# Four edits to a four-layer graph network on one core: fixed PSUM banks in attention, blocks prepared later, last rows tile by tile, source scores on the sync queue

## The chip, the cores and the metric

The kernel runs on one core of a Trainium2 chip. The metric is the device time of one execution in microseconds (us). The engines are named as in the profile: PE (matmuls; PEld is its loading of weights), DVE (vector), ACT (scalar), POOL (GpSimd) and SP (sync). SP, ACT and Pool issue DMAs; an engine issues in program order, so an instruction that waits on an engine's sequencer holds all that are behind it there.

## What is computed

`x` is 4096 x 256 and `adj` 4096 x 4096, all f32. Four layers follow each other, each with a residual and a layernorm:

```python
x = layernorm(x + attention(x, adj))   # 4 heads of 64: softmax(q k^T * 64**-0.5 + gb * adj, masked where adj == 0) v, then Wout, bout
x = layernorm(x + gat(x, adj))         # Wh = x W; e = leaky(es[i] + ed[j], 0.2), masked where adj <= 0; softmax(e) Wh
x = layernorm(x + (d adj d x) W2^T + b2)   # d = rowsum(adj)**-0.5
x = layernorm(x + relu((d adj d x) W3))
```

In layer 1, es = Wh a[:256] is the score of the source (the row) and ed = Wh a[256:] that of the target.

## The kernel before, in words

**Order of the work.** The program fixes the order of instructions on each engine (a manual schedule): every engine works through its instructions as the Python code issues them. Waits between engines and on DMAs are put in from the tiles that are read and written.

**Layer 0** takes the span from 72 to 1290 us. It goes through 64 units: 32 blocks of 128 rows, each with two pairs of heads. A unit has eight scores and eight turns, which `section` issues by the string `ORDER = "HHTHTHTTHHTHTHTT"` (L43). H is `score` (L447): for 512 columns, one matmul for each of the two heads (PE L451, with K of 64, into two PSUM banks; the profile has an f32 matmul as two records, so four for a score), and DVE L459 evicts each bank, adding the bias (edges and mask) and taking the maximum `mx` as it goes. T is `turn` (L482): 16 transposes on PE (L489) of 1024 columns of the unit *before* into two banks, which ACT L496 evicts. After the fourth H, `sums` (L515) takes the reciprocal of the exponentials' sums (DVE L519), transposes it (L527) and sends it through DRAM by two DMAs on Pool. `maxima` ends the section. Then `columns` (L600) issues what goes by unit or block: `begin` (L390, q of the next block), `finish` (L417, the output projection of the block before), `spread`, `attend` (L501; PE L505, 32 matmuls of 128 columns for each of the two heads, into the bank `po`), the exponentials (`expo`, ACT L474) and `make_bias` of the next block (DVE). `scale` (L557), first in a section, takes the result of `attend` of the unit before the last out of `po`.

PSUM has eight banks. Seven (`NB`) go round: `next_bank` (L228) and `next_two` (L233) hand them out in a fixed rotation to scores, turns, `begin` and `finish`. The eighth is `po` (L220), for `attend` alone. The last unit is turned in `drain` (L800), outside of `section`.

**Layer 1** lies between about 1314 and 1795 us. It has 32 units of 128 rows, each in four steps: 128 steps in all. A step has 32 rows, whose 4096 columns lie as four quarters of 1024 on the 128 partitions. `gat_step(t)` (L1080) issues for step t: the score of step t (DVE: `mask_out` L174 on the mask, from unit 1 on, then L996, which adds ed and takes the maximum), the leaky function of step t-2 (ACT L1008, with `es_q` as its bias), the exponential of t-5 (ACT L1037), the turn of t-6 (DVE L1045, a 32 x 32 transpose) and the attention of t-10 (`attend`, PE L1056: eight accumulating matmuls of 257 columns, 16 records, 3.47 us on PE). Every fourth step also folds the maxima of a unit (ACT L1015, DVE L1020 to L1027, ACT L1034). In its first steps PE has project_w (L176: Wh and the scores; PE L182, ACT L190 copies the result out), which a table `filling` (L1144 to L1158) spreads over steps 1 to 8. The same table has at steps 2, 5, 7 and 10 `take_es` (L192; DVE L193 copies source scores to `esd`) and `send_es` (L1119): it stores a part of `esd` to DRAM (`e_src`, L1121) and loads it back in another layout to the four quarters of `es_q` (L1123, four DMAs, which read what the store wrote). At step 5 `load_rows` (L1128) loads x into `xc` (8 x 512 KB, SP), and from step 4 on, each unit's `load_masks` (L158; L164, 8 x 128 KB, SP) is issued as the unit begins, at t = 4u. `load_last_weights` is at step 12. SP waits only for buffers to come free and for data that it reads, so these loads run ahead of the steps as far as the buffers allow.

**Layers 2 and 3** (about 1795 to 2609 us) multiply by adj in 64 steps each (`T1` = 64; 16 for each of four column blocks). A step has seven products (`product`, PE L1255, 14 records, 6.01 us a step), of sums and differences of blocks: `sums(t+1)` makes those of adj one step ahead (DVE L1199 to L1202, 2.94 us), and `prepare(p, layer)` (L940) those of x for a pair p of row blocks: layernorm (DVE L149), scaling (ACT L947), sums (DVE L950, L953, L954). When a column block ends, `keep` evicts seven banks, `combine` (L1266) adds them up on DVE in the next two steps, and `hidden_sums` (L1294) does sums on Pool. A table `at_step` gives the steps of these. For layer 3, `prepare(p, 1)` is put at the later of two steps: r0 + 4 + s, when the rows of p are through layer 2, and `free` = 48 + p + 6, when the storage that it writes is free; so p = 10 and 11 come at steps 64 and 65 and p = 12 at step 73.

**The end** (`end`, L1355) is the last column block: after the last products, eight tiles of 128 rows (n = 0 to 7) are multiplied by W3 (`weigh`, two halves f), put through relu (ACT L1383), added to x (`onto_x`, L1385), given statistics (`stats`), rates (`rates`, L1412, four tiles together), applied (`apply`) and stored in four DMAs (`put`, L1407).

Of the kernel before, what the change touches and what calls it, by code (L numbers as in the profile page):

```python
# [17 lines left out]
P = 128  # L18
# [22 lines left out]
MASK0 = -1.0e9  # L41
NB = 7
ORDER = "HHTHTHTTHHTHTHTT"  # L43

MASK1 = -4.5e16
SLOPE = 0.2
# [3 lines left out]
def tile_gnn(  # L50
# [165 lines left out]
    with ExitStack() as l0:  # L216
        ps = ExitStack()
        ps_b = ps.enter_context(tc.tile_pool(name="l0banks", bufs=1, space=PSUM))
        banks = [ps_b.tile([P, BJ], F32, name=f"bank{b}") for b in range(NB)]
        po = ps_b.tile([P, BJ], F32, name="po")  # L220

        rp = l0.enter_context(tc.tile_pool(name="l0raw", bufs=2))
        big = l0.enter_context(tc.tile_pool(name="l0big", bufs=1))
# [90 lines left out]
        class Rows:  # L314
# [73 lines left out]
                nc.sync.dma_start(self.xr, x[i0 : i0 + P, :])  # L388

            def begin(self):  # L390
                pq = next_bank()
                self.qT = wk2.tile([P, 2, P], F32, tag="qT", name="qT")
                for pr in range(2):
                    for cc in range(2):
                        for j in range(2):
                            h = 2 * pr + j
                            nc.tensor.matmul(  # L397
                                pq[j * HD : (j + 1) * HD, pr * P : (pr + 1) * P],
                                wq_sb[:, cc, h * HD : (h + 1) * HD],
                                self.xq[:, cc, :],  # L400
                                start=(cc == 0),
                                stop=(cc == 1),
                            )
# [11 lines left out]
                nc.gpsimd.tensor_tensor(self.xr, self.xr, bout_b, ALU.add)  # L415

            def finish(self):  # L417
                pp = next_bank() if self.ib + 1 < NCH else banks[NB - 1]
                for pr in range(2):
                    for j in range(2):  # L420
                        nc.tensor.matmul(  # L421
                            pp[j * HD : (j + 1) * HD, 0:D],
                            self.oT[:, pr, j * HD : (j + 1) * HD],
                            wout_sb[:, pr, :],
                            start=(pr == 0),
                            stop=(pr == 1),
                        )
                nc.vector.tensor_reduce(
                    rowsum[:, self.ib : self.ib + 1], self.rs, AX.X, ALU.add
                )  # L430
                nc.vector.tensor_tensor(self.xr, pp[:, 0:D], self.xr, ALU.add)
                ln_stats(wk2, self.xr, self.ib)
                if self.ib + 1 < NCH:
                    nc.sync.dma_start(x0_pre[self.ib * P : (self.ib + 1) * P, :], self.xr)

        class Unit:
# [7 lines left out]
                self.nm = wk2.tile([P, 2], F32, tag="nm", name="nm")  # L444
                self.ls = wk2.tile([P, 2], F32, tag="ls", name="ls", bufs=3)

            def score(self, m):  # L447
                ps = next_two()
                m0 = m * BJ
                for j in range(2):  # L450
                    nc.tensor.matmul(  # L451
                        ps[j],
                        self.rows.qT[j * HD : (j + 1) * HD, self.pr, :],
                        kT[j * HD : (j + 1) * HD, self.pr, m0 : m0 + BJ],
                        start=True,
                        stop=True,
                    )
                for j in range(2):
                    nc.vector.tensor_tensor_reduce(  # L459
                        self.z[j][:, m0 : m0 + BJ],  # L460
                        ps[j],
                        self.rows.bias[m0 // TS][:, m0 % TS : m0 % TS + BJ],
                        1.0,
                        NEG,
                        ALU.add,
                        ALU.max,
                        self.mx[:, j, m : m + 1],
                    )
# [10 lines left out]
                    accum_out=self.ls[:, j : j + 1],  # L479
                )  # L480

            def turn(self, k, j, by_dve=False):  # L482

                pa = next_two()
                z = self.z[j][:, k * TS : (k + 1) * TS]
                for c in range(CS):
                    for r in range(2):
# [13 lines left out]
            def attend(self, c0=0, c1=NCH):  # L501
# [10 lines left out]
                if c1 == NCH:  # L512
                    self.z = None

            def sums(self):  # L515

                u = self.u
                l2 = wk2.tile([P, 2], F32, tag="l2", name="l2")
                nc.vector.reciprocal(l2, self.ls)  # L519
# [53 lines left out]
        def section(u):  # L573
# [5 lines left out]
            h = t = 0  # L579
            if u >= 2:  # L580
                units.pop(u - 2).scale()
            for op in ORDER:
                if op == "H":
                    unit.score(h)
                    if h == 3:
                        before.sums()
                    h += 1
                else:
                    before.turn(t % NS, t // NS)
                    if t == 3:  # L590
                        give_edges()
                    t += 1
# [207 lines left out]
        def drain():  # L800
# [1 line left out]
            unit = units[last]  # L802

            def turn(k, j):
                unit.turn(k, j, by_dve=(j == 0))

            units[last - 1].scale()
            turn(0, 0)
            turn(1, 0)
            turn_part(0)  # L810
            load_part(7)
            unit.sums()
            rows[-1].add_bout()
            turn(0, 1)
# [36 lines left out]
        if True:  # L851
# [24 lines left out]
            load_next(0, 0)  # L876
            units[0] = Unit(0)
            for m in range(NH):
                units[0].score(m)
                if m < NH - 2:  # L880
                    project_v(m)
                if m % 2 == 0 and m < NH - 2:
# [92 lines left out]
    with ExitStack() as l1:  # L975
# [142 lines left out]

        def send_es(b0, b1):  # L1119

            nc.gpsimd.dma_start(e_src[:, b0:b1], esd[:, b0:b1])  # L1121
            for q in range(NA):
                nc.gpsimd.dma_start(  # L1123
                    es_q[q * QB : (q + 1) * QB, :, b0:b1],
                    e_src.rearrange("(a r) b -> r a b", r=QB)[:, :, b0:b1],
                )
# [49 lines left out]
    with ExitStack() as l2:  # L1176
# [51 lines left out]
        class Block:  # L1228
# [126 lines left out]
            def end(self, t0):  # L1355
# [23 lines left out]
                def onto_x(n):  # L1379
# [1 line left out]
                    ci = h * NP + self.jb * NSJ + s  # L1381
                    r = wk.tile([P, D], F32, tag="relu", name="relu")
                    nc.scalar.activation(r, py[n][:, 0:D], AF.Relu, scale=d3[:, ci : ci + 1])  # L1383
                    eng = nc.vector if n > NSJ and n % 2 else nc.gpsimd
                    eng.tensor_tensor(xc[:, ci, :], xc[:, ci, :], r, ALU.add)  # L1385

                def stats(n):
# [56 lines left out]
                for n in range(NSJ):  # L1444
                    onto_x(n)
                    stats(n)
                for n, tag in zip(range(NSJ, 2 * NSJ), ("m6", "m1", "m5", "y")):
                    weigh(n, tag, (0,))
                rates(0)
                for n in range(NSJ, 2 * NSJ, 2):  # L1450
                    for i in range(n, n + 2):
                        weigh(i, None, (1,))
                        onto_x(i)
                    stats(n)
                    stats(n + 1)
# [29 lines left out]
        with tc.manual_schedule():  # L1485
# [5 lines left out]
            for t in range(n_all):  # L1491
# [20 lines left out]
                if c == NP - 1:  # L1512
# [72 lines left out]
```

## Time and profile before

| what | us |
|---|---|
| runs | 2630.45, 2631.6, 2631.25 (median 2631.25) |
| profiled execution | 2627.84 |
| its span | 2626.1 |
| mean granted clock of PE | 0.999 |
| layer 0's units | 72 to 1290, 19.45 each |
| layer 1's steps | 1314 to 1795 |
| layers 2 and 3 | 1795 to 2609 |

The span is the time from the first to the last instruction or transfer that the profile records; the execution's own time is 1.7 us longer. The profile is one execution, by itself 3.4 us faster than the median of the runs. How to read its views:

- Busy time: each engine's busy microseconds, their share of the span and the number of instructions.
- Chain: the work that ended last, followed back from the end, at each step to what released it; a piece is its start, its length up to the start of the next piece, and engine, tile and line.
- Waits: who waited for whom, in us in all, how often, and the longest.
- Timeline: start, length, engine, line, operation, tiles (written <- read), shape, how many; in brackets the idle time before and what ended it. SPq and ACTq are DMA issues of these engines' sequencers.
- DMA issues: who issues, how many, the size of each and the median time from issue to landing, such as these of before:

```profile
mk<-edge SPq DMA_DIRECT2D x256, 128.0 KB, 2.9
x_pre<-xr SPq DMA_DIRECT2D x31, 128.0 KB, 1.7
es_q<-e_src POOLq DMA_DIRECT2D x8, 2.0 KB, 5.1
e_src<-esd POOLq DMA_DIRECT2D x2, 2.0 KB, 5.0
```

### The profile page before, as it was taken

What the parts mean: (1) busy time and instruction counts of PE and PEld (TensorE: products, weight loads), DVE (VectorE), ACT (ScalarE), POOL (GpSimd) and SP (SyncE); (2) the same over time, 40 slices, a digit from 0 to 9 for tenths busy, and PEclk for the clock granted to TensorE, in tenths of its full rate; (3) what the DMA queues carried; (4) which work ended last, traced back from release to release, by engine and by line L of the source; (5) the groups of instructions that cost most, each with busy time, mean ns of one, the idle gap of its engine ahead of it and who ended that gap; (6) DMA issues with size and microseconds to landing.
All of it is one profiled execution on the core that took longest, in us unless ns stands there. A gap on an engine that the chain in (4) does not pass through costs nothing.

```text
span 2626.1 us, 59453 instructions
## 1 busy us (share of the span) xinstructions
PE 2612.5 (99%) x24058; PEld 1829.7 (70%) x24058; DVE 2203.3 (84%) x4709; ACT 1555.6 (59%) x2195; POOL 471.6 (18%) x743
## 2 busy tenths in 40 slices
PE   9999999999999999999999999999999999999998
PEld 5777778778787787777888888885444444444444
DVE  5999999999999999999789898886966688777676
ACT  2999999999999999999877667661100001010011
POOL 0122221221222212212720000001222021121120
PEclk9999999999999999999999999999999999999999
DMA  6444544545545445454472222213544545445543
GB/s 159 89 99 91 103 94 96 102 92 98 97 94 99 97 95 103 90 100 95 155 206 76 73 78 81 73 65 113 176 158 163 170 154 172 160 160 189 173 160 111
DMA packets 678292, 312.39 MB, mean 119 GB/s; under 512 B 552096, under 2 KB 582688, under 8 KB 678016
## 3 DMA queue, kind: packets, MB, share of 16 engines
q1 hardware_dynamic: 655968, 264.97, 40.3%
q0 software_dynamic: 20096, 42.05, 4.9%
q8 instruction: 188, 3.08, 0.5%
q10 hardware_dynamic: 1952, 1.58, 0.2%
q14 instruction: 88, 0.72, 0.1%
HBM read 262.40 MB, written 46.09 MB: 117 GB/s over the span
## 4 chain that ended last, share of the span: by engine, by line
PE 98%; DVE 1%; DMA 0%; ACT 0%; POOL 0%; issue 0%; DVEq 0%; POOLq 0%; ACTq 0%
PE m L1255 29%; PE bank L451 18%; PE po L505 17%; PE po L1056 17%; PE bank L489 10%; PE py L1305 2%; PE bank L397 1%; PE bank L421 1%; PE bank L298 1%; PE bank L277 1%; PE sc L182 0%; DMA e_src<-esd 0%; DMA es_q<-e_src 0%; PE ped L744 0%; PE po L268 0%; PE py L1286 0%
## 5 line engine op out<-in xcount | busy, mean ns | idle before, releaser
L459 DVE CUSTOM_DVE_ANT_0 z<-bank,bias 128x512 f32<-128x512 f32 x1024 | 646.4, 687 | 53.5 <-PE bank L451 49.6
L496 ACT COPY z<-bank 128x512 f32<-128x512 f32 x1016 | 535.1, 598 | 109.5 <-PE bank L489 102.3
L451 PE MATMUL bank<-store,qT 64*128 64x512 f32 x2048 | 535.4, 619 | 0.0
L474 ACT ACTIVATE z<-z,nm 128x4096 f32<-128x4096 f32 x128 | 475.7, 3738 | 1.1 <-DVE nm L471 1.1
L489 PEld LDWEIGHTS bank<-ident,z 64*128 64x128 f32 x8192 | 338.1, 139 | 178.4 <-issue 136.0
L505 PE MATMUL po<-z,xc 128*64 128x128 f32 x8192 | 458.4, 273 | 0.0
L505 PEld LDWEIGHTS po<-z,xc 128*64 128x64 f32 x8192 | 450.2, 137 | 4.8
L1056 PE MATMUL po<-store,pt 128*128 128x257 f32 x2048 | 445.3, 379 | 0.0
L1056 PEld LDWEIGHTS po<-store,pt 128*128 128x128 f32 x2048 | 387.5, 189 | 57.7
L1255 PE MATMUL m<-asum,ysum 128*128 128x512 f32 x672 | 324.8, 592 | 1.9 <-DVE asum L1199 1.9
L489 PE MATMUL bank<-ident,z 64*128 64x64 f32 x8192 | 318.8, 222 | 0.7 <-DVE xt L695 0.3
L1255 PEld LDWEIGHTS m<-asum,ysum 128*128 128x128 f32 x672 | 127.6, 190 | 162.5 <-issue 144.5
L451 PEld LDWEIGHTS bank<-store,qT 64*128 64x128 f32 x2048 | 168.0, 187 | 76.2 <-issue 54.9
L1255 PE MATMUL m<-asum,store 128*128 128x512 f32 x448 | 210.7, 592 | 0.0
L1255 PE MATMUL m<-a,ysum 128*128 128x512 f32 x448 | 210.6, 592 | 0.0
L1045 DVE STREAM_TRANSPOSE pt<-z 128x1024 f32<-128x1024 f32 x128 | 158.1, 1237 | 37.9 <-PE po L1056 32.3
L1199 DVE TENSOR_TENSOR asum<-a,a 128x512 f32<-128x512 f32 x128 | 93.4, 730 | 105.7 <-PE m L1255 105.7
L374 POOL DMA_DIRECT2D edge<-mk x128 | 74.0, 578 | 578.1 <-ACT mk L368 565.4
L354 DVE SCALAR_TENSOR_TENSOR bias<-rt,gb,u 128x1024 f32<-128x1024 f32 x128 | 164.5, 1285 | 4.5
L1318 ACT COPY e<-py 128x512 f32<-128x512 f32 x28 | 16.4, 586 | 250.1 <-PE py L1305 172.9
L339 DVE STREAM_TRANSPOSE rt<-raw 128x1024 f32<-128x1024 f32 x128 | 158.6, 1239 | 5.9 <-DMA raw<-in_adjT 5.5
L1200 DVE TENSOR_TENSOR asum<-a,a 128x1024 f32<-128x1024 f32 x128 | 162.2, 1267 | 0.0
(201 smaller groups left out, 2774.6 us busy)
## 6 DMA issues: line engine op xcount, KB each, us to landing
a<-in_adjT SPq DMA_DIRECT2D x256, 512.0 KB, 4.8
raw<-in_adjT SPq DMA_DIRECT2D x512, 128.0 KB, 3.9
edge<-mk POOLq DMA_DIRECT2D x128, 256.0 KB, 3.2
mk<-edge SPq DMA_DIRECT2D x256, 128.0 KB, 2.9
xq<-in_xT SPq DMA_DIRECT2D x32, 128.0 KB, 3.6
xr<-in_x SPq DMA_DIRECT2D x32, 128.0 KB, 3.7
x<-xs POOLq DMA_DIRECT2D x8, 512.0 KB, 6.1
xc<-x SPq DMA_DIRECT2D x8, 512.0 KB, 10.1
```

The lines of the kernel that those rows point to most:

```text
L339: nc.vector.transpose(rt.rearrange("p (b r) -> p b r", r=QB), self.raw.pop(k))
L354: nc.vector.scalar_tensor_tensor(b, self.turned[0], gb, self.u, ALU.mult, ALU.add)
L451: nc.tensor.matmul(ps[j], self.rows.qT[j * HD : (j + 1) * HD, self.pr, :], kT[j * HD : (j + 1) * HD, self.pr, m0 : m0 + BJ], start=True, s ...
L459: nc.vector.tensor_tensor_reduce(self.z[j][:, m0 : m0 + BJ], ps[j], self.rows.bias[m0 // TS][:, m0 % TS : m0 % TS + BJ], 1.0, NEG, ALU.add ...
L474: nc.scalar.activation(self.z[j], self.z[j], AF.Exp, bias=self.nm[:, j : j + 1], accum_out=self.ls[:, j : j + 1],)
L489: nc.tensor.transpose(pa[r][:, c * HD : (c + 1) * HD], z[half, c * P : (c + 1) * P], ident[half, half],)
L496: copy(z.rearrange("p (c r i) -> p r c i", r=2, i=HD)[:, r, :, :], pa[r].rearrange("p (c i) -> p c i", i=HD),)
L505: nc.tensor.matmul(po[j * HD : (j + 1) * HD, 0:P], v_sb[:, ci, h * HD : (h + 1) * HD], self.z[j][:, ci * P : (ci + 1) * P], start=(ci == 0 ...
L1045: nc.vector.transpose(self.pt[:, :, s, :], self.z[:, s, :].rearrange("p (b r) -> p b r", r=QB))
L1056: nc.tensor.matmul(self.po[:, 0 : D + 1], self.pt[:, b, :, :].rearrange("p s i -> p (s i)"), wh[:, b, :], start=(b == 0), stop=(b == NBK - 1),
L1200: nc.vector.tensor_tensor(s[:, 0:2, :], a0, a1, ALU.add)
L1255: nc.tensor.matmul(self.m[i], left, right, start=(c == 0), stop=(c == NP - 1))
```

## The change

1. Layer 0: `po` becomes the eighth of `banks`. The 16 operations of a section take their two banks from a table, `PLACES`; `begin` and `finish` take bank 6 (`SIDE`), except `begin` of the first block. The first unit and `drain` keep the rotation of seven. The reciprocal of `sums` becomes a method of its own, `reciprocals`, issued after the second H.
2. Layer 3's `prepare` that `free` would put on steps 64 to 66 comes three steps later, at 67 and 68 (p = 10 and 11; p = 12 stays at 73, the later of its two steps).
3. `end`: tiles 4 to 7 are weighed one after the other with both halves, instead of all first halves and then the second ones; only tile 7 is added to x on DVE, 5 goes to Pool like 4 and 6; rates, applies and stores are in another order, and the last store, on ACT's queue, has tiles 0 and 1 of the second half instead of 2 and 3.
4. `send_es` issues its store and its four loads on SP instead of Pool.

Lines of the new kernel are 6 to 18 higher. The diff, cut to its core:

```diff
+PO = 7
+PLACES = (
+    (5, 0), (3, 6), (4, 1), (2, PO), (5, 0), (3, 4), (1, 6), (2, 5),
+    (0, PO), (1, 3), (2, 4), (5, 0), (6, PO), (1, 2), (5, 3), (4, 0),
+)
+SIDE = 6
...
+        banks.append(po)
...
             def begin(self):
-                pq = next_bank()
+                pq = banks[SIDE] if self.ib else next_bank()
...
             def finish(self):
-                pp = next_bank() if self.ib + 1 < NCH else banks[NB - 1]
+                pp = banks[SIDE]
...
-            def score(self, m):
-                ps = next_two()
+            def score(self, m, ps):
...
-            def turn(self, k, j, by_dve=False):
-
-                pa = next_two()
+            def turn(self, k, j, pa, by_dve=False):
...
+            def reciprocals(self):
+                self.l2 = wk2.tile([P, 2], F32, tag="l2", name="l2")
+                nc.vector.reciprocal(self.l2, self.ls)
...
-            for op in ORDER:
+            for op, place in zip(ORDER, PLACES):
+                to = [banks[b] for b in place]
                 if op == "H":
-                    unit.score(h)
+                    unit.score(h, to)
+                    if h == 1:
+                        before.reciprocals()
                     if h == 3:
                         before.sums()
                     h += 1
                 else:
-                    before.turn(t % NS, t // NS)
+                    before.turn(t % NS, t // NS, to)
...
         def send_es(b0, b1):
 
-            nc.gpsimd.dma_start(e_src[:, b0:b1], esd[:, b0:b1])
+            nc.sync.dma_start(e_src[:, b0:b1], esd[:, b0:b1])
             for q in range(NA):
-                nc.gpsimd.dma_start(
+                nc.sync.dma_start(
...
-                    eng = nc.vector if n > NSJ and n % 2 else nc.gpsimd
+                    eng = nc.vector if n > NSJ + 2 else nc.gpsimd
...
-                for n, tag in zip(range(NSJ, 2 * NSJ), ("m6", "m1", "m5", "y")):
-                    weigh(n, tag, (0,))
+                weigh(4, "m6")
+                onto_x(4)
+                weigh(5, "m1")
+                onto_x(5)
                 rates(0)
-                for n in range(NSJ, 2 * NSJ, 2):
-                    for i in range(n, n + 2):
-                        weigh(i, None, (1,))
-                        onto_x(i)
-                    stats(n)
-                    stats(n + 1)
+                stats(4)
                 apply(0, 0, True)
+                weigh(6, "m5")
+                onto_x(6)
+                stats(5)
+                weigh(7, "y")
+                onto_x(7)
                 apply(0, 1, True)
                 put(0, 0, nc.sync)
-                rates(1, ((0, 2, False), (0, 3, True)))
+                stats(6)
+                stats(7)
+                apply(0, 3, True)
+                rates(1, ((0, 2, False),))
                 put(0, 2, nc.sync)
-                for s in (3, 0, 1, 2):
-                    apply(1, s, s == 3)
-                put(1, 0, nc.sync)
-                put(1, 2, nc.scalar)
+                apply(1, 2, False)
+                apply(1, 3, True)
+                put(1, 2, nc.sync)
+                apply(1, 0, False)
+                apply(1, 1, False)
+                put(1, 0, nc.scalar)
...
                             free = (NJB - 1) * NP + p + NSJ + 2
+                            if T1 <= free < T1 + 3:
+                                free += 3
                             at_step(max(r0 + NSJ + s, free), "end", prepare, p, 1)
```

More of the change, by code (lines that the diff above doesn't have):

```diff
@@ L513, in attend @@
                     self.z = None
+            def reciprocals(self):
+                self.l2 = wk2.tile([P, 2], F32, tag="l2", name="l2")
+                nc.vector.reciprocal(self.l2, self.ls)
             def sums(self):
-                u = self.u
-                l2 = wk2.tile([P, 2], F32, tag="l2", name="l2")
-                nc.vector.reciprocal(l2, self.ls)
+                u, l2 = self.u, self.l2
                 if u == n_units - 1:
@@ L804, in turn @@
             def turn(k, j):
-                unit.turn(k, j, by_dve=(j == 0))
+                unit.turn(k, j, next_two(), by_dve=(j == 0))
             units[last - 1].scale()
@@ L811, in drain @@
             load_part(7)
+            unit.reciprocals()
             unit.sums()
@@ L878, in tile_gnn @@
             for m in range(NH):
-                units[0].score(m)
+                units[0].score(m, next_two())
                 if m < NH - 2:
```

## The prediction, made before the changed kernel ran

> **What bounds the kernel now.** I read the page first: the engines' busy time and the chain of work that ended last.
>
> ```profile
> PE 2612.5 (99%) x24058; PEld 1829.7 (70%) x24058; DVE 2203.3 (84%) x4709; ACT 1555.6 (59%) x2195; POOL 471.6 (18%) x743
> PE 98%; DVE 1%; DMA 0%; ACT 0%; POOL 0%; issue 0%; DVEq 0%; POOLq 0%; ACTq 0%
> ```
>
> PE is the bound from end to end, and no edit takes a matmul away. So only the places count where PE stands or is slowed, and new ones. A "busy" PE can hide waits, as matmul ends are modelled. I therefore read the chain inside one unit of layer 0, where each piece runs from its start to the next start (start, length, what).
>
> ```profile
> 616.23 1.92 PE bank L451 x8
> 618.15 0.49 PE bank L489 x16
> 618.64 0.91 PE bank L451 x4
> 619.55 0.49 PE bank L489 x14
> 620.04 0.99 PE bank L451 x4
> 621.03 0.99 PE bank L489 x32
> ```
>
> Lines 3 and 5 are the same work, a score, yet the fourth score (620.04) takes 0.99 us and the third 0.91. The waits view has who holds it:
>
> ```profile
> PEld bank L451 <- DVE mx L459: 19.9, 63, 0.3
> ```
>
> The 63 waits are those of weight loads, so part of their 19.9 us lies under running matmuls.
>
> **Part 1, fixed banks in layer 0.** In the rotation of seven, the fourth and eighth score of a unit take a bank that DVE's fourth (twelfth) eviction has only just left: in this unit it ends at 619.85. From start to next start, over the 61 units that are alike, such a score takes 0.962 us against 0.914, and the turn ahead of it 0.526 (0.521) against 0.491. That is 2 x (0.048 + 0.035) = 0.166 per unit; other pairings of the same starts give 0.147 to 0.174. With the new places these scores take a bank that was left one eviction (0.61 us) earlier, and the tightest meeting that I find (the bank of the last turn) has 0.04 to 0.15 us to spare. The eighth bank is free from `scale` on, which is first on DVE in a unit. The reciprocal moves past four evictions on DVE and is needed by nobody there. Next late would be DVE or ACT: in the unit from 609.24 to 628.69 (19.45 us) they are busy 17.71 and 17.75, so 0.17 fits. 63 units x 0.166 = **-10.4** (-9.3 to -11.0). If another bank wait takes its place, the gain is 0; a rival below.
>
> **Part 2, source scores through the sync queue.** Layer 1 starts at 1316. I read SP's and Pool's issues there, then DVE, ACT and PE.
>
> ```profile
> 1301.70 14.10 SPq L164 DMA_DIRECT2D mk<-edge  x16
> 1316.09 12.83 SPq L1131 DMA_DIRECT2D xc<-x  x8
> 1329.01 12.99 SPq L164 DMA_DIRECT2D mk<-edge  x16
> ```
>
> ```profile
> 1328.93 0.55 POOL L1121 DMA_DIRECT2D e_src<-esd  x1
> 1334.62 2.21 POOL L1123 DMA_DIRECT2D es_q<-e_src  x4 [5.14 <-DMA e_src<-esd]
> ```
>
> ```profile
> 1328.46 0.17 DVE L193 COPY esd<-store 128x4 f32<-128x4 f32 x1 [1.15 <-ACT store L190]
> ...
> 1329.68 0.42 DVE L174 TENSOR_SCALAR mk<-mk 128x1024 bf16<-128x1024 bf16 x1
> ```
>
> ```profile
> 1342.87 2.01 PE L182 MATMUL sc<-w_sb,xt 128*128 128x257 f32 x8 [1.16 <-ACT store L190]
> 1344.71 1.90 PE L182 MATMUL pm<-w_sb,xt 128*128 128x257 f32 x8
> 1346.45 3.64 PE L182 MATMUL sc<-w_sb,xt 128*128 128x257 f32 x16
> 1349.92 50.38 PE L1056 MATMUL po<-store,pt 128*128 128x257 f32 x231
> ```
>
> Now SP runs far ahead: the masks of units 1 to 3 and the rows are issued long before use, and nothing stands behind Pool's 5.14 us wait but Pool. Afterwards SP's order is: masks 0, source scores A (one store, then four loads that wait for it), masks 1, scores B, rows (8 x 512 KB), scores C, masks 2, scores D, masks 3. Queued behind each wait on SP are the masks that DVE needs next, and behind DVE's scores its turns, which attention on PE needs.
>
> What goes: ACT's wait of 1.95 us for es_q at 1341.19 and the PE stall of 1.16 behind it.
>
> What comes, in times of this trace. I take 1.8 us for a small transfer on SP (nearest row: 128 KB stores x_pre<-xr on SP land in 1.7; the other end is 5.4, Pool's e_src), 0.36 per issue, 0.46 per mask issue, 2.4 to 2.9 for a mask to land (minimum and median of L164), 354 GB/s for the rows (the 512 KB loads of xs land 1.48 apart).
> - *Masks 1.* e_src A leaves at 1328.7 and lands 1330.5; es_q issues end 1332.0; half the masks are issued by 1333.9 and landed 1336.3. DVE wanted them at 1329.68: 6.6 late. Followed through DVE's and ACT's order (scores, maxima, exponentials, the copies that free the projection's banks) and with the 1.16 gone, attention begins at 1354.7, not 1349.92: +4.9.
> - *Masks 2.* esd B is ready at 1340.1, rows go out from 1343.5, and 4.19 MB / 354 GB/s = 11.8 us fill the rings to about 1358.5. Scores C queue behind: landed 1358.8, es_q 1360, masks 2 landed 1364.6. That transfers on a queue wait so is in the trace: masks issued right behind the rows at 1329.01 took 9.2 us instead of 2.4. DVE is ready at 1351; turn 3 ends at 1368.1, and ACT frees the last projection's copy about then. PE has done attentions 0 to 2 by 1365 and goes on at 1369.2: +4.0.
> - *Masks 3.* esd D comes in DVE's order behind that, 1372.6; stored 1374.5, loaded 1376, masks landed 1380.1; turn 6 ends at 1383.6, where PE had finished at 1379.6: +4.1.
>
> The sum is **+13.0**. Varying one price at a time gives 8.5 (1.5 us, 400 GB/s, fast masks) to 17.5 (2.5 us, masks 4.4, 240 GB/s). After this PE leads again: a step has 3.47 us of PE and 3.25 of DVE.
>
> PE stands near 4 us twice. The trace has one idle stretch long enough: the granted clock is 1.00 until 2622.5 and 0.50 from 2622.7 on, 5.2 us after the last matmul; stalls of 1.2 to 1.9 show no drop. I add 0.5 for wake-ups. The Trainium skill ("TensorE: Matmul & The Clock Gate", Part 1: The HAM clock gate) puts the gate at an idle window of about 3.4 us and as long to recover; by it each stall could add some 1.7 us, an estimate of that page, and the sum would be up to 3 higher.
>
> For this edit speaks the skill's page "DMA: Bandwidth & Descriptors" (Issuing engine by pattern), which calls the sync and scalar queues generally faster than GpSimd's; the rows agree (2.4 to 2.9 against 5.0 us). Its section on the anatomy of one DMA speaks against: a semaphore wait is spent on the issuing sequencer, before dispatch; Pool's 5.14 us row shows just that. By the first alone the edit would save some 2 us, by the second it costs what is worked out above.
>
> **Part 3, blocks prepared three steps later.** At the turn from layer 2 to 3 the block for step 64 is prepared on DVE while Pool runs hidden_sums; its operations, elsewhere 0.42 and 0.28, take 1.48 and 1.35, and the sums for the next step come late:
>
> ```profile
> 2216.89 1.48 DVE L953 TENSOR_TENSOR ysum<-store 128x256 f32<-128x256 f32 x1
> 2218.29 1.35 DVE L954 TENSOR_TENSOR ysum<-store 128x128 f32<-128x128 f32 x1
> ```
>
> ```profile
> 2220.30 1.13 PE L1255 MATMUL m<-asum,ysum 128*128 128x512 f32 x2 [1.85 <-DVE asum L1199]
> ```
>
> That step takes 8.41 instead of 6.01 us. At the new steps 67 and 68 DVE has 2.94 + 2.5 = 5.4 of 6.0 us, with no hidden_sums beside it: **-2.2** (-1.9 to -2.4).
>
> **Part 4, last rows tile by tile.**
>
> ```profile
> 2622.43 0.40 ACTq L1407 DMA_DIRECT2D out_x<-ob  x1
> ```
>
> This last store's issue follows DVE, which from 2617.36 to 2622.34 runs almost without a gap: two additions onto x (0.69, 0.40), statistics of four tiles, the rates, four applies. In the new order one addition (0.40) goes to Pool and the rest stays, so the last issue comes at about 2621.9; landing (2.7) stays. **-0.5** (-0.8 if a gap of 0.3 closes too, +0.3 if Pool's addition, 0.72 to 0.8 long, holds up the statistics).
>
> **Sum.** -10.4 + 13.0 + 0.5 - 2.2 - 0.5 = +0.4 on the profiled execution's 2627.84 (span 2626.1), so 2628.2. The three runs' median, 2631.25, is 3.4 above it; against that, 2631.6.
>
> **Rivals.**
> - *The waits on SP overlap (faster, 0.18).* If small transfers and masks pass the rows instead of queuing, and masks 2 and 3 are there in time, only the first stretch stays: -10.4 + 4.9 - 2.2 - 0.5 = -8.2, 2623.0. For it: several transfers are in flight on a queue at once. Against it: the 9.2 us row.
> - *Small transfers are as slow on SP as on Pool (slower, 0.13).* At 4 us each instead of 1.8, every chain grows by two round trips and the walk gives +23: 2641.5. It decides from about 3 us each, where the sum passes +5.3. For it: 4.3 to 7 us in Pool's rows of these very transfers, but for the last four loads (1.9). Against it: SP's rows.
> - *The bank waits only change place (slower, 0.07).* The places leave 0.04 us at one turn, and DVE delivers evictions in strict order; if 0.17 us are lost elsewhere in each unit, -10.4 is 0 and the time 2642. That the change doesn't do what it says in layer 0 is this case too.
>
> **How the numbers follow.** The forecast, the terms as above, has 0.62 and its own range 2627 to 2637 (source scores 8.5 to 17.5, the rest at its bounds). Together with the faster case that is 0.80: range 2622 to 2638. A measurement of this kernel can tell about 0.2%, 5.3 us, from no change: 2626.0 to 2636.5. Faster: 0.18 and 0.03 of the forecast's lower edge. Slower: 0.13 + 0.07 and 0.03 of its upper edge. Within: 0.56.
>
> **What would show it.** Units of layer 0 at 19.28 us and no wait of L451's weight loads for mx: part 1 right. On SP at 1320 to 1380, DMA waits ahead of es_q; masks landing after DVE is idle for them; PE idle before attentions 0, 3 and 6 of 4 to 5 us: part 2 right; without the second and third, the faster rival. No long step at the turn of layers 2 and 3, last store 0.5 nearer to the last matmul: parts 3 and 4. It is wrong if masks 1 are not late, or a layer 0 unit keeps its 19.45.

## The result, and the profile after

The changed kernel takes 2644.46 us (median of 4 runs, 2644.06 to 2646.29), the kernel before on the same chip 2631.43: +13.0 us, a ratio of 1.0051 with a 95% interval of 1.0034 to 1.0069. The forecast was 2631.6 with a range up to 2638.0; the time lies above the range. The page of the changed kernel first: busy times and the chain by engine.

```profile
PE 2609.3 (99%) x24058; PEld 1805.7 (68%) x24058; DVE 2189.3 (83%) x4708; ACT 1556.1 (59%) x2195; POOL 461.3 (17%) x724
PE 97%; DMA 1%; DVE 1%; SPq 0%; issue 0%; ACT 0%; ACTq 0%; DVEq 0%
```

PE's matmuls are as many as before, 24058. On the chain DMA has grown from 0 to 1% and SP's sequencer is new: some work that PE waits for is now late in being loaded.

To find the place, I compare the same events in both traces (start of the first matmul of each, for the last score of its last matmul, us from the start of the span):

| event | before | after | difference |
|---|---|---|---|
| unit 1 of layer 0 | 72.12 | 76.47 | +4.4 |
| last score of layer 0 | 1286.95 | 1281.74 | -5.2 |
| attention step 0 of layer 1 | 1349.92 | 1366.00 | +16.1 |
| attention step 3 | 1360.36 | 1378.21 | +17.9 |
| attention step 6 | 1370.79 | 1391.73 | +20.9 |
| product step 60 | 2174.50 | 2195.44 | +20.9 |
| product step 72 | 2254.58 | 2273.12 | +18.5 |
| end of the span | 2626.07 | 2644.50 | +18.4 |

(The profiled execution, 2646.29, is the slowest of the four. Of the 4.4 us at its start about 2 are the banks', and the rest goes with the first loads; both follow under e3 and e4.) Layer 0's units gain 9.3 (the fourth score, in the chain inside the same unit, now takes 0.91 us like the third, where it took 0.99):

```profile
619.68 0.49 PE bank L494 x14
620.17 0.91 PE bank L457 x4
621.08 0.99 PE bank L494 x31
```

The turn from layer 2 to 3 gains 2.4, and between the last score of layer 0 and attention step 6 there are 26.1 lost. That stretch on PE, in the timeline of the changed kernel:

```profile
1329.15 1.90 PE L188 MATMUL pm<-w_sb,xt 128*128 128x257 f32 x8
1336.28 6.62 PE L188 MATMUL sc<-w_sb,xt 128*128 128x257 f32 x16 [5.23 <-ACT store L196]
...
1349.69 3.64 PE L188 MATMUL sc<-w_sb,xt 128*128 128x257 f32 x16
1366.00 15.85 PE L1067 MATMUL po<-store,pt 128*128 128x257 f32 x64 [12.68 <-issue]
1384.70 55.67 PE L1067 MATMUL po<-store,pt 128*128 128x257 f32 x255 [2.85 <-DVE pt L1056]
```

Three stalls, of 5.23, 12.68 and 2.85 us: in the projection, ahead of attention step 0, and ahead of step 4 (a step has 16 records). The 16 matmuls after the first stall take 6.62 us where the same 16 take 3.64 at 1349.69. What DVE was doing (its timeline, same kernel):

```profile
1346.34 1.25 DVE L1056 STREAM_TRANSPOSE pt<-z 128x1024 f32<-128x1024 f32 x1 [1.18 <-ACT z L1048]
1362.49 0.43 DVE L180 TENSOR_SCALAR mk<-mk 128x1024 bf16<-128x1024 bf16 x1 [14.91 <-DMA mk<-edge]
...
1364.68 1.23 DVE L1056 STREAM_TRANSPOSE pt<-z 128x1024 f32<-128x1024 f32 x1
```

DVE stands 14.91 us for masks 2; then comes turn 3 (1364.68), which ends at 1365.9, and 0.1 us later attention step 0 begins. SP's timeline shows why the masks are late:

```profile
1324.95 0.34 SPq L1132 DMA_DIRECT2D e_src<-esd  x1
1326.38 1.74 SPq L1134 DMA_DIRECT2D es_q<-e_src  x4
1328.29 3.59 SPq L170 DMA_DIRECT2D mk<-edge  x8
1336.69 0.34 SPq L1132 DMA_DIRECT2D e_src<-esd  x1
1338.12 1.73 SPq L1134 DMA_DIRECT2D es_q<-e_src  x4
1339.94 7.44 SPq L1142 DMA_DIRECT2D xc<-x  x8
1347.48 1.37 SPq L1132 DMA_DIRECT2D e_src<-esd  x1
1356.03 1.75 SPq L1134 DMA_DIRECT2D es_q<-e_src  x4
1357.82 3.72 SPq L170 DMA_DIRECT2D mk<-edge  x8
1370.33 0.34 SPq L1132 DMA_DIRECT2D e_src<-esd  x1
```

Each store of scores waits for DVE's data, each four loads for the landing of the store, and masks and rows stand behind both. A store takes 1.4 us, but the third, issued at 1347.48 behind the rows, lands 8.5 us later, at 1356.02, just after the last of the rows (1355.84). The granted clock (last but two of the columns) over these stalls, in windows of the changed kernel; the columns are window, length, busy time of PE, PEld, DVE, ACT and Pool, clock, DMA share, GB/s:

```profile
1334.00:1336.00 2.00, 0.00 (x0) 0.00 (x0) 1.90 (x7) 0.94 (x4) 0.00 (x0) 0.83 0.00 0
1336.00:1342.00 6.00, 5.72 (x13) 4.54 (x14) 3.42 (x7) 5.97 (x8) 0.10 (x1) 0.50 0.11 17
...
1366.00:1369.00 3.00, 3.00 (x7) 2.44 (x8) 2.93 (x5) 3.00 (x5) 0.00 (x0) 0.50 0.01 3
```

By the profile's records of the granted clock it falls to half 4.3 us into the first stall, at 1335.33, and 2.5 us into the second, at 1355.81. It stays there for 6.83 and 13.65 us, in the last 5.9 and 3.5 of which PE is back at work.

### The profile page after: what moved, and what is told of

Read it like the earlier page. It is cut to its first block, busy times and chain, and to the rows that moved or that the text cites. A ratio compares the mean times of both kernels' runs of the same rounds, so it can differ in the third digit from the quotient of the medians.

```text
span 2644.5 us, 59495 instructions
## 1 busy us (share of the span) xinstructions
PE 2609.3 (99%) x24058; PEld 1805.7 (68%) x24058; DVE 2189.3 (83%) x4708; ACT 1556.1 (59%) x2195; POOL 461.3 (17%) x724
## 4 chain that ended last, share of the span: by engine, by line
PE 97%; DMA 1%; DVE 1%; SPq 0%; issue 0%; ACT 0%; ACTq 0%; DVEq 0%
PE m L1266 29%; PE bank L457 18%; PE po L510 17%; PE po L1067 16%; PE bank L494 9%; PE py L1316 2%; PE bank L428 1%; PE bank L404 1%; PE bank L305 1%; PE bank L284 1%; PE sc L188 1%; DMA e_src<-esd 0%; DMA mk<-edge 0%; DMA w_sb<-in_wqkv 0%; PE py L1297 0%
## 5 line engine op out<-in xcount | busy, mean ns | idle before, releaser
L465 DVE CUSTOM_DVE_ANT_0 z<-bank,bias 128x512 f32<-128x512 f32 x898 | 573.0, 686 | 61.3 <-PE bank L457 42.2
L501 ACT COPY z<-bank 128x512 f32<-128x512 f32 x953 | 504.4, 598 | 103.4 <-PE bank L494 96.0
L457 PE MATMUL bank<-store,qT 64*128 64x512 f32 x1796 | 528.9, 613 | 0.0
L494 PEld LDWEIGHTS bank<-ident,z 64*128 64x128 f32 x7688 | 318.1, 139 | 198.6 <-issue 133.9
L1067 PEld LDWEIGHTS po<-store,pt 128*128 128x128 f32 x2048 | 388.5, 190 | 74.3 <-issue 16.3
L1007 DVE CUSTOM_DVE_ANT_0 z<-mk,ed_b 128x1024 f32<-128x1024 bf16 x128 | 157.1, 1227 | 4.4
```

The costliest lines, as they stand in the source:

```text
L457: nc.tensor.matmul(ps[j], self.rows.qT[j * HD : (j + 1) * HD, self.pr, :], kT[j * HD : (j + 1) * HD, self.pr, m0 : m0 + BJ], start=True, s ...
L465: nc.vector.tensor_tensor_reduce(self.z[j][:, m0 : m0 + BJ], ps[j], self.rows.bias[m0 // TS][:, m0 % TS : m0 % TS + BJ], 1.0, NEG, ALU.add ...
L494: nc.tensor.transpose(pa[r][:, c * HD : (c + 1) * HD], z[half, c * P : (c + 1) * P], ident[half, half],)
L501: copy(z.rearrange("p (c r i) -> p r c i", r=2, i=HD)[:, r, :, :], pa[r].rearrange("p (c i) -> p c i", i=HD),)
L1067: nc.tensor.matmul(self.po[:, 0 : D + 1], self.pt[:, b, :, :].rearrange("p s i -> p (s i)"), wh[:, b, :], start=(b == 0), stop=(b == NBK - 1),
```

## The experiments

The theory after the result: the whole loss is the chain of source scores on SP, by what stands behind its waits. The rival: the scores cost the 13.5 us of the forecast, and the rest comes from the other edits or from how they meet. Ratios are against the kernel before, measured on the same chip (median 2629.04 to 2630.18). "Point" is a number in the list of the change; the prediction's parts are numbered otherwise (its part 2 is point 4, its parts 3 and 4 are points 2 and 3).

**e1: the scores back on Pool, the rest of the change kept.**

```diff
-            nc.sync.dma_start(e_src[:, b0:b1], esd[:, b0:b1])
+            nc.gpsimd.dma_start(e_src[:, b0:b1], esd[:, b0:b1])
             for q in range(NA):
-                nc.sync.dma_start(
+                nc.gpsimd.dma_start(
```

> The changed kernel with send_es back on Pool's queue, the other three edits kept. Theory (the whole loss is the chain of source scores on SP ahead of the masks, 26.1 us between the end of layer 0 and attention step 6 in the two traces): 2644.5 - 26.1 = 2618.4, 13.0 below the kernel before. Rival (the scores cost the 13.5 that were forecast, the rest comes from the other edits or from their meeting): 2631.

Measured: 2620.95 against 2629.63, -8.7 us, ratio 0.9965 (0.9953 to 0.9978). By the differences to before it is 21.7 below the changed kernel; the theory had 26.1, the rival 13.5. Part of what is missing is in the trace: on Pool the wait for the store was 6.53 us in the profiled execution,

```profile
1332.20 1.12 POOL L1134 DMA_DIRECT2D es_q<-e_src  x2 [6.53 <-DMA e_src<-esd]
```

PE stood 1.88 us for it (1.16 in before), and the 8 matmuls after that took 3.69 us, not 1.90, at a halved clock. So e1 pays for the scores too, 2.5 us more than before does. In the traces the stretch from the last score to attention step 6 takes 83.8 us in before, 110.0 in the changed kernel and 88.7 in e1: 21.3 below the changed kernel, near the 21.7 of the times. The other 2.3 of its 4.8 above before lie in `drain`: a wait of 1.2 (e3), and 1.2 by a halved clock after it.

**e2: the kernel before, with only the scores on SP.** The diff is point 4 of the change alone.

> The kernel before with send_es on the sync queue and nothing else. Theory: 2631.4 + 26.1 = 2657.5, with PE idle about 5 us in the projection and about 12 us ahead of the first attention, and matmuls at half the granted clock after both. Rival: + 13.5, 2645.

Measured: 2653.62 against 2629.63, +24.0 us, ratio 1.0091 (1.0075 to 1.0106). PE's timeline has the same three stalls:

```profile
1340.60 5.28 PE L182 MATMUL sc<-w_sb,xt 128*128 128x257 f32 x16 [5.19 <-ACT store L190]
...
1370.53 16.09 PE L1056 MATMUL po<-store,pt 128*128 128x257 f32 x64 [14.22 <-issue]
1389.16 11.11 PE L1056 MATMUL po<-store,pt 128*128 128x257 f32 x50 [2.54 <-DVE pt L1045]
```

This edit alone costs all of the loss and more, as the theory had it; the rival falls. The theory's 26.1 was 1.6 too high, since that much is lost in `drain` (e3); in the traces the same stretch is 24.7 longer than in before.

**e3: the kernel before, with only the fixed banks.** The diff is point 1 of the change alone.

> The kernel before with the fixed banks and the earlier reciprocal alone. Theory (0.15 us saved in each of 62 units; once 1.9 us lost in the first block, where the fixed bank of begin meets the rotation's bank of the last project_v): -9.3 + 1.9 = -7.4, 2624.0. Rival (part of the loss is in layer 0, or its gain is lost at the hand-over to layer 1): 2629 to 2632.

Measured: 2622.76 against 2629.63, -6.9 us, ratio 0.9973 (0.9962 to 0.9984). The units' mean distance is 19.282 us against 19.432, in this kernel and in the changed one alike. At the start PE's timeline has the meeting of banks:

```profile
69.18 1.99 PE L305 MATMUL bank<-wkv_sb,x_in 128*128 128x256 f32 x8
72.80 1.99 PE L305 MATMUL bank<-wkv_sb,x_in 128*128 128x256 f32 x8 [1.63 <-DVE qT L412]
```

`begin` of the second block has taken bank 6 by the table; `project_v` takes 5 and 6 by the rotation, and waits until DVE has read q out of 6. At the other end, in `drain`, PE waits longer for DVE's copy of the first turn:

```profile
1291.05 0.22 PE L494 MATMUL bank<-ident,z 64*128 64x64 f32 x1
1291.87 0.87 PE L494 MATMUL bank<-ident,z 64*128 64x64 f32 x16 [0.61 <-DVE z L501]
```

There 0.5 to 1.3 us more than before are lost in the traces with the new banks (1.6 in the changed kernel's), behind DVE's `scale`: the second of the two loads of its input rb landed 5.9 us after its issue instead of 2.5. It goes out after SP's first 512 KB loads of xs here; in before it went ahead of them. Whether these loads are the cause was not tried.

**e4: as e1, with the banks renamed** so that the first section goes on where the rotation stood.

```diff
-    (5, 0), (3, 6), (4, 1), (2, PO), (5, 0), (3, 4), (1, 6), (2, 5),
-    (0, PO), (1, 3), (2, 4), (5, 0), (6, PO), (1, 2), (5, 3), (4, 0),
+    (1, 2), (3, 4), (5, 6), (0, PO), (1, 2), (3, 5), (6, 4), (0, 1),
+    (2, PO), (6, 3), (0, 5), (1, 2), (4, PO), (6, 0), (1, 3), (5, 2),
 )
-SIDE = 6
+SIDE = 4
...
-                pq = banks[SIDE] if self.ib else next_bank()
+                pq = banks[SIDE] if self.ib > 1 else next_bank()
```

> As e1_pool_scores (scores on Pool), with the banks of the table renamed (5 to 1, 0 to 2, 6 to 4, 4 to 5, 1 to 6, 2 to 0, so the same distances), SIDE = 4, and begin of the second block of rows on the rotation as before the change, so that project_v and begin don't meet in one bank at the start. Theory (that meeting costs 1.9 us once): 1.9 below e1, about 2619.0 where e1 has 2620.95, 10.6 below the kernel before. Rival (DVE is late there anyway and the next section waits instead): no difference from e1.

Measured: 2619.61 against 2629.04, -9.4 us, ratio 0.9961 (0.9947 to 0.9975). The wait at `project_v` is gone from the trace. By time it is 0.7 below e1, too near for the intervals to tell; by the traces, unit 1 starts at 72.1 to 73.9 us in the six kernels without that meeting (mean 72.9) and at 73.8 to 76.5 in the six with it (mean 75.0), about 2 us apart. The spread inside each group goes with the first loads: in the changed kernel's profiled execution the weights of q landed at 10.8 us, in that of before at 8.1. Where they landed alike, at 7.8 to 8.1, unit 1 starts at 72.1 to 72.6 without the meeting and at 73.8 to 74.3 with it, 1.7 apart.

**e5: the kernel before, with only the later blocks.** The diff is point 2 of the change alone.

> The kernel before with the two prepared blocks three steps later and nothing else. Theory: the long step of 8.41 us is gone, -2.4, 2629.0. Rival (the block's later preparation makes another step late, or the difference of the traces there was chance): 0, 2631.4.

Measured: 2626.91 against 2629.63, -2.7 us, ratio 0.9986 (0.9977 to 0.9994). It was forecast by the theory at -2.4. The step that took 8.41 us has no stall left (PE's timeline):

```profile
2219.30 1.02 PE L1255 MATMUL m<-asum,ysum 128*128 128x512 f32 x2
2220.16 1.88 PE L1255 MATMUL m<-asum,store 128*128 128x512 f32 x4
```

**e6: the kernel before, with only the new end.** The diff is point 3 of the change alone.

> The kernel before with the last rows tile by tile and nothing else. The traces so far have 14.27 to 14.52 us from the last product of layer 3 to the end of the span without this edit and 13.94 to 14.38 with it. Theory: 14.1, 0.2 gained. Rival (the forecast): 13.8, 0.5 gained. Neither shows in the time of one run.

Measured: 2630.0, beside 2630.18 of before. From the last product to the end of the span 13.96 us, 14.29 in before; but to the issue of the last store 10.46 against 10.65, and the rest is its landing. The issue line is this:

```profile
2624.72 0.40 ACTq L1407 DMA_DIRECT2D out_x<-ob  x1
```

So 0.2 us is the edit's own, as the theory had it: to that issue it takes 10.45 or 10.46 us in all eight traces with this edit and 10.64 or 10.65 in the four without, while the landing varies from 3.5 to 3.9.

**e10: the changed kernel without load_rows**, so that only small transfers and masks are on SP there.

```diff
-        filling[5].append((load_rows,))
```

> The changed kernel with load_rows left out: x is not loaded again for layer 1, so its residual is wrong data of the same size. Theory (masks 2 wait for scores C, whose store queues 8.5 us behind the rows): that store lands in 1.4 us, masks 2 some 7.1 us earlier, attention begins 7.1 earlier, the whole 7 us faster than the changed kernel, about 2637.5; the first stall of 5.2 us stays as it is. Rival (transfers of a queue don't wait for each other, so the rows cost nothing): 2644.

Measured: 2636.98 (one run), 7.9 above before on the same chip where the changed kernel is 13.0 above; by the bare times, from two chips, 7.5 below it. The traces tell more: from the last score of layer 0 to attention step 6 it takes 102.8 us where the changed kernel takes 110.0, 7.1 less, as worked out. SP's and DVE's timelines, and PE's:

```profile
1342.66 0.34 SPq L1132 DMA_DIRECT2D e_src<-esd  x1
1344.10 2.68 SPq L1134 DMA_DIRECT2D es_q<-e_src  x4
1346.89 3.67 SPq L170 DMA_DIRECT2D mk<-edge  x8
```

```profile
1353.68 1.23 DVE L1056 STREAM_TRANSPOSE pt<-z 128x1024 f32<-128x1024 f32 x1
```

```profile
1355.01 16.77 PE L1067 MATMUL po<-store,pt 128*128 128x257 f32 x64 [4.09 <-issue]
```

The store of scores C now takes 1.4 us, not 8.5. And attention step 0 again begins 0.1 us after turn 3 has ended (1354.9).

**e7: the scores on the scalar queue.**

```diff
-            nc.sync.dma_start(e_src[:, b0:b1], esd[:, b0:b1])
+            nc.scalar.dma_start(e_src[:, b0:b1], esd[:, b0:b1])
             for q in range(NA):
-                nc.sync.dma_start(
+                nc.scalar.dma_start(
```

> The changed kernel with the scores on the scalar queue. Theory (a wait on an engine's queue holds what stands behind it there): masks and rows are in time again, but each sending holds ACT for the store's landing (1.4) and four issues (1.7), about 3 us four times, in a stretch where ACT frees PE's banks: 2 to 8 us above e1, so 2623 to 2629. Rival (small stores and loads on a hardware queue cost 20 us by themselves): 2640 or more.

Measured: 2628.34 (one run). The masks are in time, but the first sending holds ACT for 5.6 us (ACT's timeline), and PE, which waits for ACT's copies, stands 2.69 and then runs at a halved clock:

```profile
1328.29 1.15 ACT L1019 ACTIVATE z<-z,es_q 128x1024 f32<-128x1024 f32 x1 [5.60 <-issue]
```

The theory's 2623 to 2629 holds. The price changes with what stands behind the wait, here ACT's own work.

**e8: the scores on SP, masks two units ahead, rows first.**

```diff
-                self.mk = load_masks(u) if u else first_mk
+                self.mk = masks_in.pop(u)
...
-                units[t // NSB] = Unit(t // NSB)
+                u = t // NSB
+                units[u] = Unit(u)
+                if u == 0:
+                    masks_in[1] = load_masks(1)
+                    load_rows()
+                if u + 2 < NCH:
+                    masks_in[u + 2] = load_masks(u + 2)
...
-        filling[5].append((load_rows,))
```

> The changed kernel, source scores still on the sync queue, but each unit's masks are issued two units earlier in program order and the rows before the first scores, so that nothing that is needed soon stands behind the scores on SP. Theory (not the sync queue's transfers cost, but what stands behind their waits): no idle PE of 5 and 12 us in layer 1, the wait for es_q of the kernel before (1.95 us on ACT, 1.16 on PE) gone as well, so 10 to 13 us below the kernel before. Rival (store and loads on the sync queue cost by themselves, wherever they stand): still over 10 us above the kernel before.

Measured: 2622.64 against 2629.04, -6.4 us, ratio 0.9977 (0.9967 to 0.9986). The stalls for masks are gone and the rival falls, but the forecast of 10 to 13 was missed: masks 2 now stood ahead of scores A and waited for a free buffer, so scores A left at 1330.45 and PE stood 3.46 us.

**e9: each transfer where its data are ready**, with e4's banks: masks 1 and rows, scores A, masks 2, scores B, scores C, masks 3, scores D.

```diff
-                self.mk = load_masks(u) if u else first_mk
+                self.mk = masks_in.pop(u) if u < NSB else load_masks(u)
...
+        def next_masks(u):
+            masks_in[u] = load_masks(u)
...
-        filling[5].append((load_rows,))
+        filling[2].append((next_masks, 2))
+        filling[7].append((next_masks, 3))
+        next_masks(1)
+        load_rows()
```

> All four edits, the banks renamed as in e4_banks_renamed, the scores on SP, and SP's order arranged so that each score transfer is issued when its data are there: masks 1 and the rows ahead of scores A, masks 2 right behind A, masks 3 behind C. In e8 the masks of unit 2 stood ahead of scores A and waited for a buffer until 1330, so es_q came late again (PE stood 3.46 us). Theory (only order on SP matters): that stall and the 1.2 to 1.9 us of the Pool version go, and with them a stretch of halved clock: 2 to 4 us below e4 (9.4 below the kernel before), so about 12 below the kernel before, 2617. Rival (what PE waits for there is the copies on ACT in any case): no better than e4, 2619.6.

Measured: 2617.74 against 2630.18, -12.4 us, ratio 0.9951 (0.9938 to 0.9965), 3.0 below e4 by the differences to before. It beats the kernel before and the changed one. Against e4 the two intervals overlap, but in the traces the stretch from the last score to attention step 6 is 84.4 us in e9 and 87.9 in e4, 3.6 less. The four stores of scores took 1.5 to 6.1 us here, and no engine but SP waited for them. PE goes through the projection and into attention without a stall, at full clock (PE's timeline):

```profile
1333.62 3.64 PE L188 MATMUL sc<-w_sb,xt 128*128 128x257 f32 x16
1337.10 1.90 PE L188 MATMUL pm<-w_sb,xt 128*128 128x257 f32 x8
1338.84 3.64 PE L188 MATMUL sc<-w_sb,xt 128*128 128x257 f32 x16
1342.31 7.98 PE L1067 MATMUL po<-store,pt 128*128 128x257 f32 x36
```

## Why the prediction was wrong, point by point

The parts are those of the prediction.

**What bounds the kernel: right.** PE has 99% in both, and only its stalls, and the clock after them, moved.

**Part 1: right in the units, short at both ends.** -10.4 was forecast (-9.3 to -11.0); the units give 0.150 each, -9.3 over 62, with the fourth and eighth scores at 0.914 as worked out. Not foreseen were the ends of the loop: some 2 us at the start, where the table meets the rotation, and 0.5 to 1.6 in `drain`, whose cause is open; so the edit is worth -6.9 by itself. The tightest meeting of 0.04 to 0.15 us had been looked for in a section in the middle alone.

**Part 2: the step that failed.** It was given +13.0 and 0.5; alone it costs +24.0. The walk along SP's queue came near: masks 1 were 6.8 us late on DVE (6.6 forecast); the store behind the rows took 8.5 us; masks 2 had their last needed piece at 1362.37, which in times of before (5.2 us of lead less) is 1367.6, forecast 1364.6; 1.6 of the 3.0 between them is `drain`'s. (Its 11.8 us for the rows do not lead from 1343.5 to 1358.5, which are 15.0 apart; in the trace the rows take 15.9 from the first issue to the last landing, so the time of landing fits and the sum behind it does not.) Two steps after it were wrong:

- *"PE has done attentions 0 to 2 by 1365 and goes on at 1369.2: +4.0."* It can't. `attend(s)` reads `pt[:, b, :, :]` for the column blocks b of step s, with all four slices that the four turns of the unit write; so attention step 0 waits for turn 3, not for turn 0. Three attentions, 10.4 us, that were to run under the wait for masks 2, stood behind it. In the trace attention step 0 starts 0.1 us after turn 3 has ended, in the changed kernel and in e2, e7 and e10 alike. ACT's copies of the last projection, the first of which ends in the changed kernel just then (1365.99), don't hold it: in e7 it starts after a stall at 1350.69, and they run from 1350.98 to 1352.54; in before it starts at 1349.92, and they run from 1349.82 to 1351.39. In before, too, turn 3 ends only 0.5 us ahead of attention 0, which could have been read in the profile (DVE's timeline of before):

```profile
1348.18 1.25 DVE L1045 STREAM_TRANSPOSE pt<-z 128x1024 f32<-128x1024 f32 x1 [0.42 <-ACT z L1037]
```

  The same misreading stands in its next line, where turn 6 lets attention 6 go: in the changed kernel PE stood ahead of step 4, the first of unit 1, which started 0.15 us after turn 7. So PE was not idle ahead of attentions 0, 3 and 6, as it had said, but in the projection and ahead of 0 and 4.
- *"I add 0.5 for wake-ups."* The granted clock fell to half in both long stalls. The 16 matmuls from 1336.28 on took 3.0 us longer, which the wait for masks 2 covers, and attention steps 0 to 2 took 1.8 longer, which nothing covers. The Trainium skill ("TensorE: Matmul & The Clock Gate", Part 1: The HAM clock gate) gives an idle window of about 3.4 us and about as long to recover, by which the forecast had put the sum up to 3 higher. The trace agrees with the length, 6.83 and 13.65 us being two and four times 3.41, and with the recovery: the clock came back at the end of the first such window in which PE worked throughout (1338.74 to 1342.16, and 1366.05 to 1369.46). It differs in what makes the clock fall: 2.5 us of standing were enough ahead of the second drop, as the last section shows.

The account, from the last score of layer 0 to attention step 6: 26.1 us, of which 1.6 are PE's wait in `drain`, so 24.5 for the scores. The walk had attention step 3 at 1369.2; less 1.6 for `drain` and in times of before, it is attention step 0 that starts then, at 1369.6. So 13.0 + 10.4 (three attentions without cover) + 0.4 + 1.8 (clock), less 1.0, since the wait for masks 3 was 3.1 and not 4.1: 24.6.

**Part 3: right.** -2.2 forecast, -2.4 in the traces, -2.7 alone (by the ratio's interval -1.6 to -6.0).

**Part 4: right in sign, half in size.** -0.5 forecast, 0.2 measured to the issue of the last store. The term was the addition of 0.40 that leaves DVE; which part of the line takes half of it back was not tried.

**The sum.** Parts alone: -6.9 + 24.0 - 2.7 - 0.2 = +14.2; together +13.0. Nothing large comes from their meeting. (The prediction's own bounds add up to 2626.0 to 2638.4 where it wrote 2627 to 2637; the time lies above both.)

**The rivals.** The time came out near that of the rival with slow small transfers (2641.5) by chance: but for the one store behind the rows they landed in 1.4 to 1.8 us on SP, as the forecast had taken them, and the price lay in PE's missing cover. The rival in which the waits overlap falls with e10: without the rows 7.1 us are saved, so transfers of one queue do stand behind each other. It isn't only that the rows keep the DMA engines busy: in the changed kernel, e2 and e9 the store that SP issued behind the rows landed 0.2 us after the last row, but in before the store that Pool issued at 1328.93, under the same rows, landed at 1334.33, ahead of the last row (1337.56). The Trainium skill says as much of the hardware queues ("DMA: Bandwidth & Descriptors", Queues, rings and completion order): each DMA engine takes descriptors in ring order; the 8.5 us of the third store against 1.4 for the others agrees.

## What to carry to other kernels

Before a DMA with a wait goes to another queue, list what that queue issues next and when each of these is needed; the queue's own speed comes second (the changed kernel and e9 use the same queue for the scores, and by their distances to before are 25.4 us apart, of which e4's banks are at most some 2). When a stall is said to be covered by work in hand, read from the code which of its inputs that work needs, all slices of a tile included. A table that replaces a rotation has to be followed through the first round, where both meet, and the last.

## What the runs showed that was not expected

- A short stall can cost double, by where it falls. In e1 PE stood 1.88 us and then ran 3.4 us at half clock; in before a stall of 1.85 us at the turn from layer 2 to 3, and in e4 one of 2.10, left the clock at 1.00. By the profile's records of the clock every stretch at half clock lasts 3.41 us or two or four times that (the one at the end of each run apart), and the stretches of one trace start whole multiples of 3.413 us apart (in the changed kernel at 1335.33, 1355.81 and 2639.22, so 6 and 376 of them). Cut into such windows, from 12 us to the last product and outside of `drain`, the traces have a drop after each window in which PE stood 1.88 us or more (1.88 in e1, 1.90 in e10, 2.33 in e7, 2.48 in the changed kernel), and none after 1.82 or less (1.82 in e6, 1.81 in e3). Stalls that lay across two windows cost no clock: 1.44 and 0.66 us in e4, 1.26 and 1.59 in the third stall of the changed kernel. In `drain` less was enough; in e3, where no stall was longer than 0.61 us, the clock went down for 3.4 us (windows of e3):

```profile
1292.00:1294.00 2.00, 1.61 (x32) 1.29 (x32) 2.00 (x4) 1.07 (x2) 2.00 (x3) 1.00 1.01 262
1294.00:1296.00 2.00, 1.74 (x36) 1.74 (x38) 1.72 (x5) 0.78 (x2) 2.00 (x2) 0.64 0.64 220
1296.00:1298.00 2.00, 2.00 (x44) 2.00 (x42) 1.70 (x3) 1.00 (x3) 1.68 (x3) 0.51 0.27 76
```

  There PE had stood 1.26 us in the window before; 1.40 in e4 and 1.57 in e1 did the same, but 1.34 in the changed kernel did not. What decides in `drain`, where PE works on transposes of 64 columns, is open; it makes some 1.2 us of difference between executions.
- What is under way matters more to a small transfer than who issues it. A store of 2 to 6 KB to DRAM landed after 1.4 us from SP in the changed kernel, with the DMA engines 5 to 7% busy, and after 1.7 and 1.8 from Pool (the last stores of e1 and e4, at 8 and 23%). With them 62 to 72% busy it took 2.9 to 6.1 from SP (e9), and 4.3 to 7.0 from Pool in before, at 65% and more. So the rows of 2.4 to 2.9 and 5.0 us, which the prediction set side by side for the two queues, don't show the queues' own speeds.
